# Layer 1 of a four-layer state-space and attention model: two states in PSUM in one step of four instead of two, with VectorE multiplying them by C

## The chip, the cores and the metric

The kernel runs on one core of one Trainium2 chip. The core has five engines that run their own instruction streams side by side and meet at semaphores: TensorE (PE, with its weight loads listed apart as PEld), VectorE (DVE), ScalarE (ACT), GpSimd (POOL) and the queue that issues DMAs (SP). The metric is the device time of one execution in microseconds (us). Everything is float32 in the part that matters here.

## What is computed

Four images of 64x64 pixels and 96 channels pass through four layers. Layers 0 and 1 are blocks built on a selective scan over the image in four directions; layers 2 and 3 are attention with a feed-forward part. Layer 1 works on the two-dimensional Fourier transform of the image, which has 33 columns of 64 values. The scan is the heart of it. In the reference it reads

```python
def step(h, inp):
    dt, Bt, Ct, ut = inp
    dA = jnp.exp(dt[..., None] * A[None])
    h = h * dA + dt[..., None] * Bt[:, :, None, :] * ut[..., None]
    y = jnp.einsum('bkdn,bkn->bkd', h, Ct)
    return (h, y)
```

For each direction, each of 384 channels and each of N = 16 states there is a running value h. At every position it is multiplied by a decay exp(dt A) and added to dt B u. The output is the sum over the 16 states of h times C, where C depends on position and state and not on the channel.

## The kernel before

**Tiling.** Channels lie on the 128 partitions, in C = 3 groups. Positions lie along the free dimension and are cut into segments. Layer 0 (configuration CFG0, KI = 1) handles two images at a time, 64 partitions each, in 8 segments of 512 positions. Layer 1 (CFG1, KI = 2) handles one image at a time, in 5 segments of 512, 512, 384, 384 and 320. The 16 states are taken in 4 quarters of 4 (index q). One `Step` (line 479) is one segment, one quarter q and one channel group c, so a segment has 12 steps, with numbers C * q + c from 0 to 11. Layer 0 has 768 steps, layer 1 has 960. The function `scans` (line 490) writes the steps of both layers one after the other, in an order written out by hand; engines run what they are given in that order.

**One step.** Its four states j = 0 to 3 take the following way:

- The decays are exponentials made by ACT (line 648): those of states 0 and 1 go to an SBUF tile `ax` one step ahead (`front_x`), those of states 2 and 3 go into PSUM banks (`front_y`).
- The inputs dt B u of states 0 and 1 are made by ACT in transposed form (`make_bx`, line 612) and turned by PE into PSUM banks (`transposed`, line 644). Those of states 2 and 3 are products made by GpSimd in SBUF, in the tile `h` (`front_b`, line 666).
- VectorE runs the recurrence with one scan instruction for each state (`scan`, line 676). A scan reads one operand from SBUF and one from PSUM. Its result goes either over its PSUM operand, if j is in `st.kept`, or to the tile `h` in SBUF.
- A kept state is multiplied by C on VectorE (`multiply_kept`, line 694), which reads PSUM and writes a tile `hk` in SBUF. ACT copies its last value to the state that the next segment begins from (`keep_state`, line 701).
- The states that are not kept lie side by side in `h`. In the next step of the order GpSimd copies their last values (line 710) and multiplies all of them by C with one instruction (`multiply`, line 713).
- PE turns each product back and sums it over states in a PSUM accumulator (`accumulate`, line 723), a kept one as soon as it is there (`add_kept`), the rest two steps later (`add_rest`).

**Buffers and order.** The tile `h` has 3 buffers, `hk` has 2. Three PSUM banks (`ab0` to `ab2`) go round among the four PSUM operands of each step. GpSimd in step i runs `multiply` of step i - 1 and then `front_b` of step i + 1, for which PE's `add_rest` of step i - 2 must have freed the buffer. PE in step i runs `add_rest` of step i - 2, `add_kept` of state 3 of step i - 1 where there is one, `add_kept` of state 0 of step i, and the transposes for step i + 1. VectorE runs scan 0, the multiply of state 0, scans 1, 2 and 3, and where state 3 is kept its multiply, directly ahead of the next step's scan 0.

**Side work.** Between the steps, at fixed slots, the loop puts pieces of other work: convolutions, projections and normalizations of the layers before and after, the Fourier transforms, and the attention layers of images that have left layer 1. It falls on all engines in bursts. The work of the last image after the scan stands alone at the end.

The rule that says which states a step keeps is set in `Step`: in both layers the first step of two keeps state 0, the second keeps states 0 and 3.

Of the kernel before, what the change touches and what calls it, by code (L numbers as in the profile page):

```python
# [22 lines left out]
C, P = 3, 128  # L23
# [7 lines left out]
class Cfg:  # L31
# [5 lines left out]
    def __init__(self, pre, NI, KI, NR, nat, R, parts, rows, segs, eps):  # L37
        self.pre = pre
        self.NI, self.PI, self.KI = NI, P // NI, KI
        self.DI = C * self.PI  # L40
        self.NR, self.L, self.nat = NR, NR * 64, nat
        self.R, self.M = R, R + 2 * NST
        self.parts = parts
        self.rows = [(sum(rows[:i]), n) for i, n in enumerate(rows)]
        self.segs = [(sum(segs[:i]), n) for i, n in enumerate(segs)]
        self.eps = eps
# [432 lines left out]
class Step:  # L479


    def __init__(self, z, q, c):
        self.z, self.q, self.c = z, q, c
        self.nm = f"{z.nm}_{q}_{c}"
        self.kept = (0, 3) if (C * q + c) % 2 else (0,)
        self.hk = {}
        self.px, self.ay = {}, {}

# [1082 lines left out]
```

## Time and profile before

| | |
|---|---|
| median of 3 runs | 11412.55 us (11408.17 to 11425.88) |
| the profiled execution's own time | 11418.96 us |
| its span in the profile | 11417.2 us |
| PE busy | 9108.9 us (80%) |
| DVE busy | 9922.7 us (87%) |
| ACT busy | 9367.1 us (82%) |
| POOL busy | 9402.0 us (82%) |

A busy share is the part of the span in which the engine executes something; an engine that is not busy waits for another engine, a buffer or a transfer. In the profile's lines a group of instructions is given as line, engine, operation, result and operands by the program's names with digits left out (so `ab_l`, `b_l` and `_l` are all PSUM banks of the steps, and `hk_l`, `k_l` the products of kept states), the count, the busy time and the mean length, and after a bar the idle time of the engine just before, with what ended it. From the scans' starts, layer 0's steps run from 214 us to 5172 us of the span, layer 1's from 5172 us to 11012 us; the stretch after it, 406 us, is the last image's rest.

### The profile page before, as it was taken

Reading aid. Unit: us, or ns where it says so; the run is one execution under the profiler, and the core shown is the slowest. Engines: PE = TensorE matmul, PEld = TensorE weight load, DVE = VectorE, ACT = ScalarE, POOL = GpSimd, SP = SyncE. Lnnn points to the kernel's source line nnn. Section 1 sums busy time; section 2 is a strip of 40 time slices with the busy share of each in tenths; the row PEclk is TensorE's granted clock in tenths of the full one; section 3 lists DMA queues with packets and bytes.
Section 4 is the critical chain, followed back from the end, with each engine's and each line's share of the span. In section 5 each row is a group of like instructions: output and inputs, shape, how many; then the busy total and the mean of one; then the engine's idle time right before and its main releaser. Section 6 shows DMA issues by size and latency. Waiting matters only on the chain. (4 is left out here: it accounts for less than half of the span.)

```text
span 11417.2 us, 163659 instructions
## 1 busy us (share of the span) xinstructions
PE 9108.9 (80%) x54944; PEld 6661.7 (58%) x54944; DVE 9922.7 (87%) x10695; ACT 9367.1 (82%) x19648; POOL 9402.0 (82%) x7464
## 2 busy tenths in 40 slices
PE   5668878788888878888888888887778877887775
PEld 2555555555666656556665565665556556665554
DVE  6889999889998998999878687988999899889964
ACT  4779999999988998998768777878888798878853
POOL 2899999988988998998779688887888788888850
PEclk9889999988998999998889899998899988998887
DMA  4555554556665455555543443542244422542242
GB/s 142 131 140 127 130 132 123 144 154 167 160 166 127 130 143 130 134 140 165 156 125 122 123 133 121 172 129 88 97 121 148 110 94 97 151 130 97 87 124 40
DMA packets 1208403, 1468.94 MB, mean 129 GB/s; under 512 B 482760, under 2 KB 1020560, under 8 KB 1149064
## 3 DMA queue, kind: packets, MB, share of 16 engines
q1 hardware_dynamic: 1207559, 1458.48, 47.0%
q8 instruction: 434, 7.11, 0.3%
q14 instruction: 410, 3.35, 0.1%
HBM read 1221.74 MB, written 236.50 MB: 128 GB/s over the span
## 5 line engine op out<-in xcount | busy, mean ns | idle before, releaser
L713 POOL TENSOR_TENSOR h_l<-h_l,bc_l 128x1536 f32<-128x1536 f32 (+2 forms) x1728 | 4565.0, 2642 | 203.2 <-DVE h_l L676 87.4
L666 POOL TENSOR_TENSOR h_l<-du_l,bc_l 128x512 f32<-128x512 f32 (+2 forms) x3456 | 3964.8, 1169 | 859.1 <-PE acc_l L723 806.4
L612 ACT ACTIVATE bx_l<-dut_l,bt_l 128x192 f32<-128x192 f32 (+2 forms) x6272 | 2750.8, 499 | 0.2
L723 PE MATMUL acc_l<-ident,h_l 128*128 128x128 f32 (+1 forms) x15840 | 2365.1, 302 | 257.0 <-POOL h_l L713 255.8
L723 PEld LDWEIGHTS acc_l<-ident,h_l 128*128 128x128 f32 (+1 forms) x15840 | 2065.1, 157 | 843.2 <-POOL h_l L713 389.5
L648 ACT ACTIVATE ax_l<-delta_l,l_alog 128x512 f32<-128x512 f32 (+2 forms) x3456 | 2140.4, 667 | 0.0
L676 DVE TENSOR_TENSOR_SCAN h_l<-b_l,state_l,h_l 128x512 f32<-128x512 f32 (+2 forms) x1266 | 1398.7, 1124 | 195.5 <-ACT b_l L648 181.7
L644 PE MATMUL b_l<-ident,bx_l 128*128 128x128 f32 (+1 forms) x6830 | 1233.9, 298 | 350.8 <-DVE h_l L676 339.4
L644 PEld LDWEIGHTS b_l<-ident,bx_l 128*128 128x128 f32 (+1 forms) x6830 | 834.8, 150 | 840.3 <-DVE h_l L676 628.3
L648 ACT ACTIVATE b_l<-delta_l,l_alog 128x512 f32<-128x512 f32 (+2 forms) x1952 | 1222.8, 626 | 102.5 <-DVE k_l L694 32.0
L644 PE MATMUL ab_l<-ident,bx_l 128*128 128x128 f32 x5320 | 916.0, 301 | 278.8 <-DVE h_l L676 265.9
L723 PE MATMUL acc_l<-ident,k_l 128*128 128x128 f32 x5121 | 838.5, 294 | 340.4 <-DVE k_l L694 323.8
L676 DVE TENSOR_TENSOR_SCAN b_l<-ax_l,state_l,b_l 128x512 f32<-128x512 f32 (+2 forms) x844 | 956.0, 1133 | 136.7 <-PE b_l L644 136.2
L648 ACT ACTIVATE ab_l<-delta_l,l_alog 128x512 f32<-128x512 f32 x1328 | 914.8, 689 | 146.3 <-DVE hk_l L694 62.5
L676 DVE TENSOR_TENSOR_SCAN h_l<-ab_l,state_l,h_l 128x512 f32<-128x512 f32 x744 | 925.3, 1263 | 113.3 <-ACT ab_l L648 64.5
L644 PEld LDWEIGHTS ab_l<-ident,bx_l 128*128 128x128 f32 x5320 | 655.4, 153 | 579.4 <-DVE h_l L676 474.2
L676 DVE TENSOR_TENSOR_SCAN h_l<-ax_l,state_l,b_l 128x512 f32<-128x512 f32 (+2 forms) x844 | 953.7, 1130 | 38.6 <-PE b_l L644 37.4
L694 DVE TENSOR_TENSOR k_l<-b_l,bc_l 128x512 f32<-128x512 f32 (+2 forms) x1462 | 896.5, 613 | 62.6 <-DMA bc_l<-l_xd_l 9.1
L723 PEld LDWEIGHTS acc_l<-ident,k_l 128*128 128x128 f32 x5121 | 632.2, 150 | 437.5 <-DVE k_l L694 356.2
L723 PE MATMUL acc_l<-ident,hk_l 128*128 128x128 f32 x3984 | 647.4, 300 | 249.6 <-DVE hk_l L694 237.7
L276 PE MATMUL pc_l<-pad_l,l_dg 128*128 128x512 f32 (+2 forms) x1656 | 771.1, 560 | 40.2 <-ACT state_l L701 22.0
L694 DVE TENSOR_TENSOR hk_l<-ab_l,bc_l 128x512 f32<-128x512 f32 x996 | 688.9, 692 | 54.5 <-issue 11.1
(252 smaller groups left out, 14802.7 us busy)
## 6 DMA issues: line engine op xcount, KB each, us to landing
bc_l<-l_xd_l SPq DMA_DIRECT2D x640, 512.0 KB
bc_l<-l_xd_l SPq DMA_DIRECT2D x512, 256.0 KB
bc_l<-l_xd_l SPq DMA_DIRECT2D x128, 1024.0 KB
bc_l<-l_xd_l SPq DMA_DIRECT2D x128, 768.0 KB
us_l<-l_u SPq DMA_DIRECT2D x96, 768.0 KB
l_y<-y_l SPq DMA_DIRECT2D x288, 256.0 KB
yt_l<-l_y SPq DMA_DIRECT2D x264, 192.0 KB
yt_l<-l_y SPq DMA_DIRECT2D x128, 384.0 KB
```

The lines of the kernel that those rows point to most:

```text
L276: nc.tensor.matmul(pc[:, : n * 64].rearrange("p (r w) -> p r w", w=64), diag[:, t, :], pad[:, r - p0 + dy : r - p0 + dy + n, dx : dx + 64] ...
L612: nc.scalar.activation(t[:n, b, :, ch], z.dut[:n, b, :, ch], AF.Copy, scale=z.bt[:n, b, m : m + 1])
L644: nc.tensor.transpose(pb[:, t : t + n], st.z.bx[st.q, j][:n, b, st.c], ident[:n, :n])
L648: nc.scalar.activation(out, z.delta[:, st.c, : z.S], AF.Exp, scale=z.blk.A[:, st.c, z.k, n : n + 1])
L666: nc.gpsimd.tensor_tensor(st.h[:, 1 + j, :S], st.z.du[:, st.c, :S], st.z.b[st.q][:, j, :S], ALU.mult)
L676: nc.vector.tensor_tensor_scan(h[:, ::step], a[:, ::step], b[:, ::step], 0.0 if z.first else z.state[st.c][:, n : n + 1], ALU.mult, ALU.add,)
L694: nc.vector.tensor_tensor(hk[:, : z.S], kept_at(st, j), z.c[st.q][:, j, : z.S], ALU.mult)
L713: nc.gpsimd.tensor_tensor(h, h, z.c[st.q][:, 1 : 1 + m, : z.S], ALU.mult)
L723: nc.tensor.matmul(z.acc[st.c][:m, b, :], hc[:, t : t + m], ident, start=(first and b == 0), stop=(last and b == 0), is_transpose=True,)
```

## The change

One line in `Step` is another. In layer 0, where KI is 1, the condition has the same value as before. In layer 1, where KI is 2, states 0 and 3 are kept in steps 1, 5 and 9 of each segment, not in steps 1, 3, 5, 7, 9 and 11. In steps 3, 7 and 11 state 3 now goes to SBUF beside states 1 and 2; GpSimd multiplies three states with its instruction in place of two and copies their last values, VectorE has no second multiply and ACT no second copy there, and PE adds state 3 in `add_rest` instead of `add_kept`. Nothing that is computed changes.

```diff
@@ -482,7 +482,7 @@
     def __init__(self, z, q, c):
         self.z, self.q, self.c = z, q, c
         self.nm = f"{z.nm}_{q}_{c}"
-        self.kept = (0, 3) if (C * q + c) % 2 else (0,)
+        self.kept = (0, 3) if (C * q + c) % (2 * z.cfg.KI) == 1 else (0,)
         self.hk = {}
         self.px, self.ay = {}, {}
 
```

## The prediction

> **What bounds the kernel now.** I read the busy shares of the page first, then the window view with the run cut at the first and last step of layer 1, then the groups by shape and the waits of that stretch, and the chain last.
>
> Columns of the window view: window, length, then busy time and count of PE, PEld, DVE, ACT, POOL, then PE clock, DMA share and GB/s. The second window is layer 0's loop of steps, the third layer 1's; two windows of one segment (12 steps) each follow in the second fence.
>
> ```profile
> 214.00:5172.00 4958.00, 3948.82 (x23692) 2916.88 (x23693) 4516.56 (x4336) 4418.38 (x9467) 4568.73 (x3367) 0.91 0.56 139
> 5172.00:11012.00 5840.00, 4791.92 (x29254) 3510.90 (x29252) 5151.15 (x5948) 4760.08 (x9761) 4813.42 (x4059) 0.89 0.41 122
> ```
>
> In layer 1 VectorE is busy 5151 of 5840 us (88%), GpSimd 4813 (82%), ACT 4760 (82%), PE 4792 (82%). No engine is full: VectorE leads by 338 us, and it is idle for 689. In layer 0 the order of the two is the other way round (GpSimd 92%, VectorE 91%).
>
> ```profile
> 5172.00:5239.00 67.00, 57.54 (x392) 44.93 (x390) 66.36 (x67) 59.82 (x115) 65.45 (x49) 0.96 0.53 168
> 8049.00:8136.00 87.00, 65.45 (x351) 49.69 (x349) 86.21 (x86) 65.84 (x116) 76.52 (x48) 0.79 0.28 95
> 8615.00:8684.00 69.00, 60.98 (x369) 43.88 (x369) 60.38 (x75) 58.19 (x120) 55.97 (x52) 0.93 0.51 156
> ```
>
> Layer 1 is a mixture. In the first segment VectorE (99%) and GpSimd (98%) are both full; in the second VectorE alone (99%, GpSimd 88%), because side work of the attention layers lies on it; in the third PE leads (88%) with matmuls of side work, and VectorE and GpSimd both wait. Cut in this way into its 80 segments, layer 1 has 15 in which GpSimd, with the work added below, would need over 98.5% of the segment's present length, 10 others with VectorE at 95% or more, and 55 in which neither holds.
>
> ```profile
> POOL h_l L666 <- PE acc_l L723: 609.7, 334, 11.9
> DVE h_l L676 <- ACT b_l L648: 131.1, 165, 3.2
> DVE b_l L676 <- PE b_l L644: 105.4, 64, 10.5
> DVE ab_l L676 <- PE ab_l L644: 81.6, 39, 11.1
> PE acc_l L723 <- POOL h_l L713: 31.7, 32, 3.0
> ```
>
> These are waits in layer 1 (total us, times, longest). GpSimd's idle time is mostly spent waiting for PE to give back an h buffer. PE hardly waits for GpSimd's multiply: 31.7 us, where the same wait in layer 0 is 224.0. VectorE waits for ACT's exponentials and PE's transposes.
>
> ```profile
> by line: DVE h_l L676 22.2%; issue 11.9%; DVE ab_l L676 10.4%; POOL h_l L713 5.6%; POOL h_l L666 4.6%; DVE b_l L676 4.6%; ACT xn L1177 4.3%; ACT ax_l L648 4.1%; ACT bx_l L612 3.3%; ACT _l L648 2.6%; DVE hk_l L694 1.9%; DVE _l L676 1.9%; POO
> ```
>
> This is the chain of waits from 10800 to 11011 us; it reaches back to about 10060. Adding its pieces from there to 11012 (952 us): scans (L676) 240 us, L694 29, L713 27, L666 23, the rest on ACT and PE. So no engine carries the end alone. L694 has 862 us in layer 1, a quarter of it (215) in the last image's 1435 us, so some 143 in 952 us: 20% of it is on the chain. L713 (2334 us, so 387) is there for 7%.
>
> **What the Trainium skill says.** "Perfetto Trace Analysis", Identifying the Most-Contended Engine, takes the engine with the highest occupancy as the one to work on: VectorE here, though the 689 us of idle warn that occupancy is an average. "GPSIMD Engine Reference", 3.1 Elementwise, says a fp32 tensor_tensor is 1.96 times slower on GpSimd; the trace has 1.09 us against 0.69 for the third state (ratio 1.57), so the transfer costs more than it frees. "SBUF — State Buffer", two separate sides, says that a VectorE operation with two SBUF inputs and a GpSimd operation lock each other out. Every scan and every L694 here reads one operand from PSUM, after the change too, and L713 of 128x1536 has one mean (3.45 us) in the whole run and in layer 1: no new lock is expected.
>
> **The change part by part.** Layer 0 has KI = 1 and keeps its rule. Layer 1 has 960 steps: 4 images, 4 directions, 5 segments of 512, 512, 384, 384, 320, 12 steps each. Of each 12, steps 1, 5, 9 keep two states and 3, 7, 11 now keep one: 240 steps change, 96 of length 512, 96 of 384, 48 of 320. The compiled order has 240 instructions fewer on VectorE, 192 fewer on ACT, as many in the same order on GpSimd, and no DMA more or less.
>
> ```profile
> L713 POOL TENSOR_TENSOR h_l<-h_l,bc_l 128x1536 f32<-128x1536 f32 x192 | 663.0, 3453 | 47.1 <-DVE h_l L676 35.4
> L713 POOL TENSOR_TENSOR h_l<-h_l,bc_l 128x1024 f32<-128x1024 f32 x193 | 456.4, 2365 | 19.3 <-DVE h_l L676 7.8
> L694 DVE TENSOR_TENSOR hk_l<-ab_l,bc_l 128x512 f32<-128x512 f32 x523 | 361.7, 692 | 18.0
> L676 DVE TENSOR_TENSOR_SCAN h_l<-ab_l,state_l,h_l 128x512 f32<-128x512 f32 x360 | 449.5, 1265 | 46.9 <-ACT ab_l L648 43.5 <-POOL h_l L713 1.6 <-POOL h_l L666 1.1
> L676 DVE TENSOR_TENSOR_SCAN ab_l<-ab_l,state_l,h_l 128x512 f32<-128x512 f32 x120 | 153.0, 1275 | 17.5 <-ACT ab_l L648 14.1 <-issue 2.4 <-POOL h_l L713 1.0
> ```
>
> VectorE loses the multiply of state 3: 96 x 692 + 96 x 558 + 48 x 492 ns (the rows of 384 and 320) = 144 us. The scan of state 3 writes SBUF instead of PSUM: 1265 against 1275 ns, 2 us in all, nothing.
>
> GpSimd gains a third of a multiply: 3453 - 2365 = 1088 ns at 512, 2633 - 1817 = 816 at 384, 2222 - 1544 = 678 at 320: 104 + 78 + 33 = 215 us. Its copy of states takes 188 ns for two or three columns.
>
> ACT loses the copy of state 3 except in each direction's last segment: 192 x 0.145 = 28 us. PE does as many transposes; four of them now wait for GpSimd (L713) instead of VectorE (L694). The PSUM bank of state 3 comes free one multiply earlier for the next step's exponential (L648), which waited 57 us for hk in layer 1.
>
> So VectorE goes from 5151 to 5007 us and GpSimd from 4813 to 5028: they change places, nearly level. For an unchanged 5840 us both would be at 86%.
>
> What of it reaches the end: the removed multiply stands directly ahead of the next step's scan 0, and it also delays ACT, so I take 25%, a little over the 20% of all L694: 36 us (bounds 15% and 50%: 22 and 72). ACT's copies: a sixth, 4 us (0 to 8). GpSimd at the 7% of L713: 15 us lost (bounds 0, if all of it goes into the 610 us in which GpSimd waits for buffers anyway, and 35%, 75 us). Behind the longer multiply stands front_b of the step after next (L666), and PE's add_rest waits for it; VectorE needs both about a step later, some 5 to 6 us, so 0.7 to 1.1 us is mostly absorbed. Sum: -36 - 4 + 15 = -25 us, against the profiled execution's 11418.96 (1.8 more than its span) 11394. That execution is 6 us over the median of the runs, 11412.55; taken off the median it is 11388, which I predict.
>
> **Rivals.** *VectorE's pace is the pace.* In the timeline of a busy stretch (start, length, engine) a step with two kept states lasts longer by the whole multiply:
>
> ```profile
> 8361.84 1.01 DVE L676 TENSOR_TENSOR_SCAN b_l<-ax_l,state_l,b_l 128x384 f32<-128x384 f32 x1
> ...
> 8366.70 0.99 DVE L676 TENSOR_TENSOR_SCAN b_l<-ax_l,state_l,b_l 128x384 f32<-128x384 f32 x1
> ...
> 8371.66 0.56 DVE L694 TENSOR_TENSOR k_l<-b_l,bc_l 128x384 f32<-128x384 f32 x1
> 8372.13 1.01 DVE L676 TENSOR_TENSOR_SCAN b_l<-ax_l,state_l,b_l 128x384 f32<-128x384 f32 x1
> ```
>
> From one scan 0 to the next are 4.86 us for the step with one kept state and 5.43 for the step with two, each with one cast of side work in it; the difference, 0.57, is the 0.56 of the multiply at 8371.66. If half of the 144 us arrives, the gain is 72 us and the time 11340. For it: the segments at 99%. Against it: 55 of 80 segments with no full VectorE, and the scans at only a quarter of the chain.
>
> *GpSimd becomes the bound (slower).* Place: segments such as the first above. There GpSimd's 65.45 us grow by 3 x 1.088 to 68.7, and at 98% busy the segment takes 70 instead of 67: +3 us. A plain stretch without side work is then GpSimd's. Over 15 or 16 such segments this floor gives only +8 to +13 us net. But if elsewhere too PE comes to wait for L713 as it does in layer 0 (224 us against 32), transposes behind it in PE's order are late, and a quarter to a third of the 215 us arrives: +54 to +70 less a gain that shrinks to about 25: +35, 11448. It decides once GpSimd's share of layer 1 rises above VectorE's with PE's waits for it. For it: 86% against 86%, and GpSimd has three long multiplies in a row before a short one. Against it: 610 us of buffer waits as slack.
>
> That gain and loss cancel exactly belongs to the likeliest case's range.
>
> **How the numbers follow.** Small gain (11388, own range 11368 to 11408) 50%; VectorE's pace (11340) 18%; GpSimd's bound (11448) 32%. Differences under 0.2%, 23 us, can't be told from none. The likeliest case lies half below 11390 and half in the band: 0.25 each. The second gives 0.17 faster, the third 0.06 in the band and 0.26 slower. Faster 0.42, same 0.32, slower 0.26. The range from 11340 to 11455 leaves out half of the second case and a third of the third.
>
> **What would show it.** Right: VectorE in layer 1 falls by about 144 us and GpSimd rises by 215; L713 of 128x1536 has 288 instructions in layer 1 instead of 192; PE's wait for L713 stays under 100 us; full-VectorE segments as at 8049 shorten by 1 to 2 us and the one at 5172 lengthens by up to 3. Wrong, if GpSimd's waits for PE vanish and PE's waits for GpSimd grow past 100 us (slower), if segments led by PE also shorten (more gain than forecast), or if L713 of 128x1536 takes more than 3.5 us.

## The result, and the profile after

The changed kernel takes 11378.42 us (median of 6 runs, 11372.74 to 11383.11) against 11417.74 us (median of 6, 11404.04 to 11428.5) for the kernel before: 39 us less, ratio 0.9964 with a 95% interval of 0.9953 to 0.9974, which is 30 to 54 us. The forecast was 25 us less. The profiled execution took 11377.41 us, with a span of 11375.6.

In the window view of the changed kernel (window, length, then busy time and count of PE, PEld, DVE, ACT, POOL, then PE clock, DMA share and GB/s), the first line is layer 1. The three after it are the segments that were shown of the kernel before, where they now lie:

```profile
5172.00:10976.00 5804.00, 4731.84 (x29245) 3485.28 (x29244) 5019.76 (x5707) 4727.70 (x9569) 5019.21 (x4057) 0.89 0.41 122
5172.00:5240.00 68.00, 53.66 (x381) 41.22 (x380) 64.35 (x63) 58.89 (x112) 66.44 (x48) 1.00 0.52 162
8040.00:8125.00 85.00, 58.30 (x346) 43.73 (x346) 83.68 (x81) 65.33 (x113) 80.73 (x48) 0.88 0.28 96
8599.00:8666.00 67.00, 59.04 (x365) 42.45 (x363) 58.95 (x73) 57.41 (x117) 58.33 (x52) 0.95 0.54 163
```

Layer 1 took 5840 us and takes 5804; layer 0, in which the change touches nothing, has the same length as before (4959 against 4958). VectorE lost 131 us in layer 1 (5151 to 5020), GpSimd gained 206 (4813 to 5019), and they are level to the microsecond. (Busy time counts stretches in which two instructions overlap once; the lengths of all instructions, added up over the whole run, fell by 147 us on VectorE and rose by 222 on GpSimd.) The segment in which both were full went from 67 to 68 us and GpSimd alone nearly fills it now (98%, VectorE 95%). The one in which only VectorE was full went from 87 to 85. The one that PE led went from 69 to 67.

Sorted by what was full in the kernel before, the 80 segments of layer 1, cut from one scan 0 to the next, changed by this much in the two traces: the 14 in which GpSimd was busy 93% or more by +6 us, 18 others with VectorE at 93% or more by -13, and the 48 in which neither was by -28. Most of the gain lies where neither VectorE nor GpSimd was full. (In 6 of the 48 PE was at 93% or more; they gave 3 of the 28.) These sums are of one trace each. In the trace of `e4` below, whose time can't be told from that of the kernel before, the 48 segments are 8 us shorter, so a few microseconds here mean nothing. Another 6 us (406 to 400) are in the stretch after layer 1, in which the change touches nothing.

The waits of layer 1 after the change (total us, times, longest):

```profile
POOL h_l L666 <- PE acc_l L723: 474.9, 257, 13.2
PE acc_l L723 <- POOL h_l L713: 155.6, 134, 3.6
DVE h_l L676 <- ACT b_l L648: 150.0, 197, 3.2
DVE b_l L676 <- PE b_l L644: 124.8, 77, 11.1
DVE ab_l L676 <- PE ab_l L644: 92.2, 51, 12.3
DVE h_l L676 <- POOL h_l L666: 59.2, 68, 3.1
```

PE now waits 155.6 us for GpSimd's multiply where it waited 31.7, and VectorE waits longer for ACT and PE than before (131.1, 105.4 and 81.6 there). GpSimd still waits 475 us for PE to return an h buffer (610 before). So much of VectorE's freed time came back as waits: its idle time in layer 1 rose from 689 to 784 us. The groups of GpSimd and VectorE at 512 positions in layer 1:

```profile
L713 POOL TENSOR_TENSOR h_l<-h_l,bc_l 128x1536 f32<-128x1536 f32 x287 | 990.5, 3451 | 47.4 <-DVE h_l L676 28.0 <-PE ab_l L644 1.8
L713 POOL TENSOR_TENSOR h_l<-h_l,bc_l 128x1024 f32<-128x1024 f32 x97 | 229.3, 2364 | 6.9 <-DVE h_l L676 1.1 <-POOL state_l L710 0.2
L694 DVE TENSOR_TENSOR hk_l<-ab_l,bc_l 128x512 f32<-128x512 f32 x435 | 300.8, 691 | 15.0
```

Counts moved as planned (287 against 192 of three states at 512; the window's edge cuts one), and the lengths did not: 3451 against 3453 ns, 691 against 692. In these rows no engine slows another one down.

### The profile page after: what moved, and what is told of

Its sections match the earlier page's. It is cut to its first block, busy times and chain, and to the rows that moved or that the text cites. A ratio compares the mean times of both kernels' runs of the same rounds, so it can differ in the third digit from the quotient of the medians.

```text
span 11375.6 us, 163430 instructions
## 1 busy us (share of the span) xinstructions
PE 9055.5 (80%) x54944; PEld 6643.2 (58%) x54944; DVE 9789.8 (86%) x10455; ACT 9333.7 (82%) x19456; POOL 9612.1 (84%) x7464
## 5 line engine op out<-in xcount | busy, mean ns | idle before, releaser
L713 POOL TENSOR_TENSOR h_l<-h_l,bc_l 128x1536 f32<-128x1536 f32 (+2 forms) x1728 | 4780.4, 2766 | 190.8 <-DVE h_l L676 72.9
L723 PE MATMUL acc_l<-ident,h_l 128*128 128x128 f32 (+1 forms) x16656 | 2459.2, 301 | 371.0 <-POOL h_l L713 369.0
L723 PEld LDWEIGHTS acc_l<-ident,h_l 128*128 128x128 f32 (+1 forms) x16656 | 2144.7, 156 | 994.3 <-POOL h_l L713 560.0
L676 DVE TENSOR_TENSOR_SCAN h_l<-b_l,state_l,h_l 128x512 f32<-128x512 f32 (+2 forms) x1389 | 1516.4, 1112 | 238.4 <-ACT b_l L648 195.6
L644 PE MATMUL b_l<-ident,bx_l 128*128 128x128 f32 x6884 | 1237.9, 297 | 337.8 <-DVE h_l L676 327.7
L644 PEld LDWEIGHTS b_l<-ident,bx_l 128*128 128x128 f32 x6884 | 844.9, 150 | 814.2 <-DVE h_l L676 601.0
L676 DVE TENSOR_TENSOR_SCAN h_l<-ab_l,state_l,h_l 128x512 f32<-128x512 f32 x804 | 998.4, 1264 | 137.3 <-ACT ab_l L648 74.4
L723 PE MATMUL acc_l<-ident,k_l 128*128 128x128 f32 x4755 | 782.0, 294 | 305.2 <-DVE k_l L694 287.8
L694 DVE TENSOR_TENSOR k_l<-b_l,bc_l 128x512 f32<-128x512 f32 (+2 forms) x1343 | 831.4, 619 | 58.1 <-DMA bc_l<-l_xd_l 8.6
L676 DVE TENSOR_TENSOR_SCAN ab_l<-ax_l,state_l,ab_l 128x512 f32<-128x512 f32 x497 | 632.8, 1273 | 122.2 <-PE ab_l L644 121.8
```

Of the source, the lines that this page charges most:

```text
L644: nc.tensor.transpose(pb[:, t : t + n], st.z.bx[st.q, j][:n, b, st.c], ident[:n, :n])
L676: nc.vector.tensor_tensor_scan(h[:, ::step], a[:, ::step], b[:, ::step], 0.0 if z.first else z.state[st.c][:, n : n + 1], ALU.mult, ALU.add,)
L694: nc.vector.tensor_tensor(hk[:, : z.S], kept_at(st, j), z.c[st.q][:, j, : z.S], ALU.mult)
L713: nc.gpsimd.tensor_tensor(h, h, z.c[st.q][:, 1 : 1 + m, : z.S], ALU.mult)
L723: nc.tensor.matmul(z.acc[st.c][:m, b, :], hc[:, t : t + m], ident, start=(first and b == 0), stop=(last and b == 0), is_transpose=True,)
```

## The experiments

The net was near the forecast; whether its terms were is another question. Theory A is the forecast's: VectorE's half of the change is worth some 40 us with ACT's, and GpSimd's half costs about 15. All ratios are to the kernel before, run on the same chip beside each kernel; microseconds are the ratio times 11416.

### The two halves alone

`e1` lengthens GpSimd's instruction in the 240 steps and leaves everything else as before. Its third product is not used.

```diff
+        self.moved = z.cfg.KI == 2 and (C * q + c) % 4 == 3
...
+        if st.moved:
+            m, h = 3, st.h[:, :3, : z.S]
         nc.gpsimd.tensor_tensor(h, h, z.c[st.q][:, 1 : 1 + m, : z.S], ALU.mult)
```

> The kernel before, except that in steps 3, 7 and 11 of layer 1's segments GpSimd's multiply takes three columns of states instead of two (the third product is not used); VectorE and ACT keep all their work. It is the GpSimd half of the change alone, 215 us of busy time. Theory A (GpSimd's longer multiply reaches the end for 7% of its length): 15 us slower than the kernel before, between 5 and 30. Rival B (it is free, hidden in waits for h buffers): within 5 us. Rival C (it costs a quarter or more, and the change gains because VectorE's half is worth much more): 50 us slower or more.

Measured: 1.0023 (1.0016 to 1.0029), 26 us slower (18 to 33). Theory A's range holds; its 15 was low, and GpSimd's time is not free.

`e2` is the changed kernel in which GpSimd multiplies two states in those steps, so that state 3 is added without its C:

```diff
+        if st.moved:
+            m, h = 2, st.h[:, :2, : z.S]
         nc.gpsimd.tensor_tensor(h, h, z.c[st.q][:, 1 : 1 + m, : z.S], ALU.mult)
```

> The changed kernel, except that in steps 3, 7 and 11 of layer 1's segments GpSimd multiplies only two of the three states by C, as before; state 3 is added without its multiplication by C there. It is the half of the change on VectorE and ACT alone. Theory A: since the change took 39 us off with GpSimd's cost of about 15 in it, this one takes 54 us off the kernel before (45 to 70). Rival B: 39 us, the same as the change. Rival C: 90 us or more.

Measured: 0.9917 (0.9904 to 0.9930), 95 us faster (80 to 110). That is far from theory A and rival B and is what rival C expected of this run (90 or more), though C's part for `e1` (50 or more slower) did not come. VectorE's half is worth more than twice what theory A gave it. The change itself stands at -41 by its ratio. So in the change GpSimd's half costs 95 - 41 = 54 us, a quarter of its 215; measured alone it costs 26. The difference, 28, is not much above the intervals of the three runs taken together (about 20), so that the cost grows as VectorE gets lighter is likely and not certain. The trace of `e2` has VectorE as in the change and GpSimd as before:

```profile
5170.00:10917.00 5747.00, 4716.13 (x29252) 3468.70 (x29251) 5006.73 (x5707) 4725.66 (x9569) 4810.73 (x4058) 0.90 0.41 124
```

Against the kernel before, its layer 1 is shorter by 22 to 23 us in each of the four images, the PE-led first one too, and PE's wait for the multiply is 65.8 us:

```profile
PE acc_l L726 <- POOL h_l L716: 65.8, 61, 3.1
```

### Further along the same way

`e3`: no step of layer 1 keeps two states.

```diff
+        self.kept = (0, 3) if z.cfg.KI == 1 and (C * q + c) % 2 else (0,)
```

> The changed kernel carried on: in layer 1 no step keeps two states; VectorE loses another 144 us, GpSimd gains another 215 (to about 5235 us, 90% of layer 1). Theory A (GpSimd is now the fuller engine and its weight on the chain grows, VectorE's falls): 10 to 40 us slower than the change, so -30 to 0 against the kernel before. Rival D (VectorE's pace is the pace throughout): again 39 us faster, -78 against the kernel before. Rival C: slower than the kernel before by 30 us or more.

Measured: 1.0014 (1.0007 to 1.0021), 16 us slower than the kernel before and so some 57 slower than the change. That is beyond theory A's span, short of rival C's 30, and far from rival D's 78 us faster; the sign is the one that the crossing of the two engines gives. Its layer 1 and two of its waits:

```profile
5168.00:11037.00 5869.00, 4729.83 (x29246) 3522.41 (x29244) 4901.29 (x5469) 4698.35 (x9377) 5228.50 (x4057) 0.89 0.40 121
PE acc_l L723 <- POOL h_l L713: 312.4, 230, 4.1
DVE h_l L676 <- POOL h_l L666: 143.3, 154, 3.9
```

GpSimd leads by 327 us. PE's wait for it is twice that of the change (155.6 us), and VectorE waits for `front_b`. The 14 segments in which GpSimd was 93% busy before are 44 us longer than in the kernel before; in the change they are 6 longer. This is the slower rival of the prediction, one dose later.

### What VectorE's half consists of

`e4`: the kernel before without ACT's copy of state 3 in those steps; the next segment's scan of it begins from state 2's last value.

> The kernel before, except that ACT does not copy the last value of state 3 in steps 3, 7 and 11 of layer 1's segments (192 copies fewer); the next segment's scan of that state begins from the last value of state 2 instead, so what is carried over for state 3 is left out. Theory A (ACT's copies are a small part of the gain): 0 to 8 us faster than the kernel before, 4 as the middle. Rival E (the copy, for which ACT stands waiting with the next step's exponentials queued behind it, is the main source): 20 to 40 us faster.

Measured: 0.9996 (0.9987 to 1.0004), 5 us, not told from none. ACT's copy is not the source of the gain.

`f1` is `e2` with VectorE's time put back at the old place, after scan 3:

```diff
+            elif st.moved:
+                hk = sp.tile([P, SM], F32, name=f"hx_{st.nm}", tag="hk", bufs=2)
+                nc.vector.tensor_tensor(hk[:, :S], st.ay[3][:, :S], z.c[q][:, 3, :S], ALU.mult)
```

> The kernel of e2_dve_alone (GpSimd multiplies two states, state 3 is added unmultiplied) with the multiply on VectorE put back as time alone: in steps 3, 7 and 11 of layer 1's segments VectorE, after scan 3, multiplies the exponential of state 3, which lies in the same PSUM bank, by C into an hk tile that nobody reads. VectorE's 144 us and the longer hold of the bank are back; PE's add_kept in its old place and ACT's copy are not. Theory A2 (the 95 us of e2 come from VectorE's time and the bank): within 20 us of the kernel before. Rival F (they come from PE, which no longer waits in its order for the product of state 3): 60 us or more faster than the kernel before remain.

Measured: 0.9961 (0.9947 to 0.9974), 45 us faster than the kernel before. Neither expectation: VectorE's time (with the longer hold of the bank) is 50 of the 95 us, and 45 (30 to 60) remain. `g4` puts ACT's copy back as well:

```diff
+            if before and before.moved and not before.z.last:
+                e = last(before.z)
+                sx = sp.tile([P, 1], F32, name=f"sx_{before.nm}", tag="sx", bufs=2)
+                nc.scalar.copy(sx, before.ay[3][:, e : e + 1])
```

> f1_dve_time_back with ACT's copy put back as time alone: ACT copies one column of the same PSUM bank into a tile that nobody reads, at the place where the kernel before copies state 3. GpSimd multiplies two states, state 3 is added unmultiplied. What is left of the difference to the kernel before is where PE adds state 3 (with h instead of hk) and where scan 3 writes. If ACT's copy is the source of what f1 left: within 12 us of the kernel before. If PE's order is: 30 to 45 us faster than it still. e4 gave 5 us for the copy alone.

Measured: 0.9952 (0.9938 to 0.9966), 55 us faster than the kernel before (39 to 71), not told apart from `f1`. So with VectorE's and ACT's time back, 45 to 55 us of the 95 remain by the ratios. The traces say less: in `f1`'s, layer 1 is 41 us shorter than in the kernel before, in `g4`'s 31, and in `e2`'s 92. In `g4`'s trace another 27 us lie in layer 0, which has the same instructions in both kernels (10 us in `f1`'s), and no run explains them.

Several differences to the kernel before are left in these runs. That scan 3 writes SBUF, and that nobody reads the stand-in's buffer, no run takes apart. One of the two that were followed up shows in the timelines (start, length, engine). The kernel before, at a scan of state 3, its multiply and the next step's scan 0:

```profile
8370.62 1.00 DVE L676 TENSOR_TENSOR_SCAN b_l<-b_l,state_l,h_l 128x384 f32<-128x384 f32 x1
8371.66 0.56 DVE L694 TENSOR_TENSOR k_l<-b_l,bc_l 128x384 f32<-128x384 f32 x1
8372.13 1.01 DVE L676 TENSOR_TENSOR_SCAN b_l<-ax_l,state_l,b_l 128x384 f32<-128x384 f32 x1
```

The same place in `f1`, with the stand-in at line 880:

```profile
8367.27 1.02 DVE L677 TENSOR_TENSOR_SCAN h_l<-b_l,state_l,h_l 128x384 f32<-128x384 f32 x1
8368.20 0.53 DVE L880 TENSOR_TENSOR hx_l<-b_l,bc_l 128x384 f32<-128x384 f32 x1
8368.65 1.01 DVE L677 TENSOR_TENSOR_SCAN b_l<-ax_l,state_l,b_l 128x384 f32<-128x384 f32 x1
```

The real multiply reads what the scan has just written and starts 0.04 us after its end. The stand-in reads the exponential, which is there already, and starts 0.09 us before the scan's end. From scan 3 to the next scan 0 are 1.51 us with the multiply and 1.38 with the stand-in; two scans in a row are about 0.93 apart. So `f1` gives VectorE back 0.45 of the 0.58 us, three quarters, and part of what remains is probably VectorE's pace after all: at `f1`'s own rate (50 us for three quarters) some 15 us. That is an estimate, not measured.

The other is where PE takes in state 3. `f2` moves the kept product's transposes one step later in PE's order, in the kernel before, with one hk buffer for each state. `g3` does it with three shared buffers:

```diff
             if older:
+                if 3 in older.kept:
+                    add_kept(older, 3)
                 add_rest(older)
             if before and 3 in before.kept:
                 keep_state(before, 3)
-                add_kept(before, 3)
```

> The kernel before, but in both layers PE adds the kept product of state 3 one step later, just ahead of add_rest of the same step, when it has long been there; hk has one buffer for state 0 and one for state 3 instead of two shared. No work is less. Theory A2 (PE's wait for the product is not what counts): within 20 us of the kernel before. Rival F: 40 us faster or more, as PE's waits for k and hk (331 us in layer 1) shrink.

> f2_add_kept_later again with three shared buffers of hk instead of one for each state, so that VectorE never waits there for PE; room from two small tiles of the attention layers that share it. Rival F (PE's wait for the product of state 3 in its old place is the other 45 us that f1 left): 25 us or more faster than the kernel before. Against it: within 12 us of the kernel before.

Measured: `f2` 1.0009 (1.0001 to 1.0017), 10 us slower; `g3` 0.9980 (0.9971 to 0.9988), 23 us faster. `f2` has a new wait that can have taken the gain away (VectorE's multiply for PE's use of the single hk buffer, in layer 1):

```profile
DVE k_l L694 <- PE acc_l L723: 30.7, 17, 8.0
```

Without that, PE's place is worth 23 us (14 to 33), between what was expected for rival F and against it. `g3` also has one hk buffer more than the kernel before, which was not run alone; the 200 longest waits of the kernel before have none of VectorE for PE's use of an hk buffer, so it is an unlikely source. The 23 us hold for 864 steps of both layers, and `g3`'s profiled layer 1 is only 5 us shorter than before. So PE's order may be a part of the rest in layer 1, and is not shown to be the whole.

### What GpSimd's half waits for

`f3`: the changed kernel with four buffers of h instead of three; other tiles made room.

```diff
-        st.h = sp.tile([P, 3, SM], F32, name=f"h_{st.nm}", tag="h", bufs=3)
+        st.h = sp.tile([P, 3, SM], F32, name=f"h_{st.nm}", tag="h", bufs=4)
```

> The changed kernel with four buffers of h instead of three in both layers (room for it from one buffer of xs instead of two, one shared tag for bt, and two small tiles that share room). GpSimd's waits for PE to give back h (475 us in layer 1) should fall. Theory G1 (GpSimd's half costs what it does because GpSimd starts late behind those waits): 20 us or more faster than the change, 60 or more than the kernel before. Theory G2 (it costs through stretches where GpSimd is full, and through PE's wait for the longer multiply itself): within 15 us of the change, about 25 to 50 us faster than the kernel before.

Measured: 0.9927 (0.9915 to 0.9940), 83 us faster than the kernel before, some 42 faster than the change. GpSimd's wait for PE is gone from layer 1 (17 us of 475), and it waits for VectorE's scans instead:

```profile
POOL state_l L710 <- DVE h_l L676: 410.8, 200, 8.1
...
PE acc_l L723 <- POOL h_l L713: 119.7, 100, 3.5
...
POOL h_l L666 <- PE acc_l L723: 17.0, 8, 7.8
```

That looks like theory G1. But `g1`, the kernel before with the same four buffers, tells otherwise:

> The kernel before with four buffers of h, by the same room as in f3_four_h. If the buffers return what GpSimd's longer multiply cost in the change (theory G1: 26 to 56 us of it), they bring less here than the 44 us that they brought to the change: 20 us or less off the kernel before. If the round of h buffers holds layer 1 up whatever the rule is (theory H), they bring 35 us or more here too, and the change would be worth about its 39 us again on top.

Measured: 0.9959 (0.9946 to 0.9971), 47 us faster. GpSimd's wait for PE is gone from layer 1 here too (16 us). The buffers bring as much without the change as with it, and on top of them the change is worth 0.9927 / 0.9959 = 0.9968, 37 us. So the round of h buffers holds layer 1 up by itself, whatever the rule (theory H), and it does not look like the reason why GpSimd's half costs 54 us; the halves were not priced apart with four buffers. In the two traces the gain of the buffers lies in the 48 segments in which neither VectorE nor GpSimd was full: -45 us in `g1` against before, -76 in `f3` against -28 in the change.

`f4`: the changed kernel with ACT instead of GpSimd copying the last values of the states not kept, in layer 1. `g2`: this and four buffers together.

> The changed kernel, but in layer 1 ACT and not GpSimd copies the last values of the states that are not kept (768 copies of about 0.19 us, some 135 us off GpSimd; ACT gains some 110 to 140), at the start of the next step. If GpSimd's time is worth the 26 to 60% that e1 and the difference of e2 and the change show, and ACT's the quarter that e4 shows, it is 5 to 45 us faster than the change, 45 to 85 faster than the kernel before. If ACT, waiting there with the exponentials behind it, is worth more: no faster than the change.

> The changed kernel with both: four buffers of h, and the copies of last values on ACT in layer 1. If the two gains over the change (44 and 25 us) come from one cause, GpSimd's late start, the sum is well short of 69: some 90 us off the kernel before. If they add, about 105 to 110.

Measured: `f4` 0.9944 (0.9932 to 0.9957), 64 us faster than the kernel before, 23 faster than the change: GpSimd's time is worth something, ACT's less. `g2` 0.9925 (0.9912 to 0.9937), 86 us, the same as `f3`: the two gains do not add. In `g2` GpSimd waits for the copies on ACT:

```profile
POOL h_l L713 <- ACT state_l L720: 448.4, 231, 12.6
```

`f3`, at 11332.25 us against 11422.85, computes the same as both kernels and is faster than both.

## Why the prediction was right, and where its terms were not

- **Counts and lengths**: as forecast. 240 multiplies of VectorE less; its instructions add up to 147 us less for 144 forecast, GpSimd's to 222 more for 215, and single lengths did not change.
- **VectorE's and ACT's time, 36 + 4 = 40 us**: `e2` less `g4` gives 95 - 55 = 40, `e2` less `f1` 50; in layer 1 of the traces it is 61 and 51. Since the stand-in gives back only three quarters of VectorE's time, the whole is some 15 us more, by estimate. So the term was of the right order and rather too small, though inside its bounds (22 to 72, and 0 to 8 for ACT). ACT's 4 us fits `e4`'s 5, which can't be told from none.
- **PE and the place of state 3, costed at nothing** ("PE does as many transposes; four of them now wait for GpSimd"): this step failed. When VectorE's and ACT's time is put back, 45 to 55 us of the gain remain by the ratios, 31 to 41 in layer 1 of the traces. Some 15 of them are, by estimate, VectorE's time that the stand-in did not give back, and belong to the row above. That the rest is PE's place in order is argued, not shown: `g3` measured 23 us for both layers, and its trace has 5 of them in layer 1. What the rest consists of stays open.
- **GpSimd's 15 us**: mis-sized. It measured 26 alone and, as a difference of two runs, 54 beside the lighter VectorE, inside the bounds of 0 and 75, though not by the mechanism that I gave. The multiply's delay was said to be mostly absorbed; PE's wait for it grew to 155.6 us, past the 100 that I had set.
- **The net**: 25 forecast, 39 to 41 measured. The gain was 55 us larger than forecast (95 against 40), the loss 39 larger (54 against 15), and the two errors mostly offset each other. That the sum came out near is luck.
- **The granted clock**: a rival that no run tests. With each run stands the share of full speed that TensorE's clock was granted. In the 77 runs of the kernel before that stand beside the experiments (0.890 to 0.898), a share higher by 0.001 goes with some 4 us less. The changed kernel's runs have 0.897 in the middle, these 0.894, so by estimate some 12 of the 39 us go with the clock. In the two traces layer 0's clock is 0.91 in both and layer 1's 0.889 before and 0.894 after, so the clock may have risen because of the change; whether it is a cause of the gain or comes with it is open.
- **Where in layer 1**: I looked for the gain in the segments with a full VectorE. They gave 13 us; those in which neither VectorE nor GpSimd was full gave 28. (My count of segments was off: from the trace, 8 and not 15 pass the mark that I set for GpSimd, and 17 others have a full VectorE; the 55 in which neither holds are right.) The forecast for single segments held (67 to 68 us where both were full, 87 to 85 where VectorE was). The sign I had listed as "more gain than forecast", shorter PE-led segments, decides nothing: the 24 segments in which PE was the busiest of the three are 14 us shorter after the change, but 13 us shorter in the trace of `e1` too, whose kernel is slower.
- **Rivals**: VectorE's pace as the only pace is refuted by `e3`. GpSimd as the bound comes true one step further, in `e3` (44 us in the segments in which GpSimd was full); in the change these segments are 6 us longer.

## What to carry to other kernels

When work moves between two engines, price each half with a run of its own: here +26 and -95 stood behind -41, and it is likely that they do not simply add. An instruction's place can count beyond its length: a stand-in of the same shape that waits for nothing gave back only three quarters of the time. A long wait for buffers is slack only as long as the round of buffers is not itself the limit; one buffer more, tried on both sides of a change, tells which.

## What the runs showed of the hardware that was not expected

On VectorE, in the steps that the change touches (240 of each), a multiply that reads the scan just before it starts 34 ns after that scan's end, by the median, while one that does not depend on it starts 83 ns before the end. The kernel before has the same 34 ns at other places where VectorE reads what the instruction just ahead wrote, outside the scans too (12 of 12 places at which `xn` is made from `lnm_2a`), and a scan that follows a scan to SBUF, on which it does not depend, starts 82 ns before its end. So with the same row a dependent neighbour takes about 0.12 us more of the engine than an independent one, which is 28 us over 240 of them.
